# A softmax in layer 0: key tiles added in pairs by DMAs, half of the sums on TensorE, reciprocals with the queries on partitions

## The chip, the cores and the metric

The kernel runs on one core of a Trainium2 chip. The metric is the device time of one execution in microseconds (us). The kernel before was run three times: 3317.89, 3320.54 and 3327.8 us, median 3320.54. One further execution was profiled; its times are the ones told below.

A core has five engines that run their own streams of instructions in order and wait for each other through semaphores: TensorE (PE; its weight loads are listed as PEld), VectorE (DVE), ScalarE (ACT), GpSimd (POOL) and SyncE (SP), which here issues DMAs.

## The reference, cut to what matters

Two layers on 8 images of 256 channels and 32 x 32 pixels. Layer 0 is an attention over the 1024 pixels with a 3x3 depthwise convolution of the values beside it, and then a gated feed-forward part with another depthwise convolution and a filter in 8x8 Fourier blocks. Layer 1 is a causal attention and a mixture of 8 experts. The change lies in layer 0's attention:

```
def _attention(x, ...):
    B, Cc, H, W = x.shape
    N = H * W                                     # 1024 pixels
    qkv = _bn(_conv1x1(x, qkv_w), ...)
    qkv = qkv.reshape(B, NH, 2 * KD + HD, N)      # 4 heads, 32 + 32 + 64 channels
    q, k, v = (qkv[:, :, :KD], qkv[:, :, KD:2 * KD], qkv[:, :, 2 * KD:])
    attn = jnp.einsum('bhkn,bhkm->bhnm', q, k) * SCALE
    attn = jax.nn.softmax(attn, axis=-1)
    out = jnp.einsum('bhdm,bhnm->bhdn', v, attn).reshape(B, Cc, H, W)
    pe = _bn(_dwconv3(v_img, pe_w), ...)
    return _bn(_conv1x1(out + pe, proj_w), ...)
```

So each output is a sum over the keys of exponentials times values, divided by the sum of the same exponentials.

## The kernel before, in words

**Attention of one image** (`attend`, L724). The scores are computed transposed: keys on partitions, queries along the row. The 1024 queries go in 4 chunks of 256 (QC), the keys in 8 tiles of 128; a chunk and a tile make one step of the loop, 32 an image, 256 in all. A step does this:

- PE multiplies the keys with the queries of each head into PSUM tile `s`, 128 x 4 heads x 256 (L793). Queries and keys are split in a high and a low part, and four combinations are stacked along the partitions in `qst` and `kst`.
- ScalarE takes the exponential into `pT` (L795), without a shift by the maximum; a test at the end of the layer tells whether that was safe.
- For the tile before, `product` (L732) multiplies `pT` with the values, 8 matmuls of 32 columns each into `po`, and with a column block of ones, 4 matmuls of 32 columns into `sums`. Four column groups lie side by side in the array, so the sums of a head come out repeated on 32 partitions.

After the 8 tiles of a chunk `close` (L750) copies `po` to `pu` and `sums` to `ss` (ScalarE), and leaves a list of steps that are taken one by one in the following steps of the loop: `invert` takes the reciprocal of all 128 x 256 elements of `ss` on VectorE, `split` copies it into a high part on ScalarE and subtracts on GpSimd for the low part, and `spread` multiplies high and low part with a selection matrix on PE (4 matmuls), so that each channel has its head's reciprocal (`rb`), then multiplies `pu` by it and adds the result to `o` on VectorE. The steps of an image's last chunk are taken in `finish` (L808).

**The rest of layer 0** runs woven into this. `main_of(i)` (L1050) gives the stream of image i: the second norm of image i-1 and the Fourier part (`spectrum`) of image i-2, woven with the first steps of `attend(i)`; then `attend(i)` woven with the norm, queries and keys of image i+1 (`queries_keys`); then `stack(i+1)`, the values of i+1 (`values`) woven with `finish(i)` and the Gelus of i-1; then the projection (`project`). Beside it, `together` (L415) lays a side stream by a ratio of estimated microseconds: `hidden`, whose 3x3 convolution is done by `tap` (L561), one `scalar_tensor_tensor` on VectorE for each of 8 taps and each channel group, with PE's `ph` and ScalarE's copies into the padded tiles `hpad`. PE, ScalarE, VectorE and GpSimd are wrapped in `InOrder`, so that each one's instructions stand in the order in which the program makes them. The DMAs are SyncE's, and a scheduler places them.

**Buffers.** `pT` has 2 buffers, `s` 2 of two PSUM banks, `po` and `sums` one each. `hi` and `lo` of queries and keys have a buffer each; `stack` (L672) copies them within SBUF by 32 DMAs of 128 KB an image, 32 partitions each.

Of the kernel before, what the change touches and what calls it, by code (L numbers as in the profile page):

```python
# [9 lines left out]
F32 = mybir.dt.float32  # L10
# [45 lines left out]
NVEC = _n  # L56

# [17 lines left out]
def conv_attn_hybrid_kernel(  # L75
# [29 lines left out]

    vec = const.tile([P, NVEC], F32, name="vec")
    nc.sync.dma_start(vec, vecs)

    def col(name, i=0, n=1):
        o, w = _VOFF[name]  # L110
        assert i + n <= w
        return vec[:, o + i : o + i + n]
# [319 lines left out]
    with ExitStack() as l0:  # L432
# [78 lines left out]
        for k in range(KC):  # L511
# [8 lines left out]
        pick_r = wpool.tile([P, NH // 2, P], F32R, name="pick_r")  # L520
        pickr = one.tile([P, NH, HD], F32, tag="full", name="pickr", bufs=2)
        nc.gpsimd.memset(pickr, 0.0)
        nc.gpsimd.affine_select(
            out=pickr, in_=pickr, compare_op=ALU.not_equal, fill=1.0, base=0,
            pattern=[[-KD, NH], [0, HD]], channel_multiplier=1,
        )
# [3 lines left out]
        pick_n = wpool.tile([2 * nq, nq, P], F32R, name="pick_n")  # L530
        pickn = one.tile([2 * nq, nq, P], F32, tag="full", name="pickn", bufs=2)
        nc.gpsimd.memset(pickn, 0.0)
        for half in range(2):
            nc.gpsimd.affine_select(
                out=pickn, in_=pickn, compare_op=ALU.not_equal, fill=1.0, base=-nq * half,
                pattern=[[-1, nq], [0, P]], channel_multiplier=1,
            )
# [8 lines left out]
        def padded(name):  # L546
            p = one.tile([P, H + 2, W + 2], F32, tag=name, name=name)
            nc.gpsimd.memset(p, 0.0)
            return p

# [3 lines left out]
        def interior(p, h):  # L554
            r = H // 2
            return p[:, 1 + h * r : 1 + (h + 1) * r, 1 : 1 + W]
# [4 lines left out]
        def tap(dst, p, w, k):  # L561
            src = p[:, k // 3 : k // 3 + H, k % 3 : k % 3 + W]
            dve.scalar_tensor_tensor(rows(dst), src, w[:, k : k + 1], rows(dst), ALU.mult, ALU.add)
# [5 lines left out]
        def rms_norm(b, wname, xn):  # L569
# [38 lines left out]
            def apply(h):  # L608
                rT = rT_of.pop(h)
                rb = ps_m.tile([P, HALF], F32, tag="mm", name="rbn")  # L610
                for i in range(nq):
                    pe.matmul(rb[:, i * P : (i + 1) * P], pick_n[:, i, :], rT, start=True, stop=True)
                hs = slice(h * HALF, (h + 1) * HALF)
                for k in range(KC):
                    dve.scalar_tensor_tensor(xn[:, k, hs], t[b][:, k, hs], col(wname, k), rb, ALU.mult, ALU.mult)
# [36 lines left out]
        def queries_keys(b):  # L652
# [7 lines left out]
            for g in range(2):  # L660
                hi = one.tile([P, N], F32R, tag=f"hi{g}", name="hi")
                lo = one.tile([P, N], F32, tag=f"lo{g}", name="lo")
                bias = qkv_o[:, g : g + 1]

                def take(hs, pq):
                    act.activation(hi[:, hs], pq, AF.Identity, bias=bias)
                    dve.scalar_tensor_tensor(lo[:, hs], pq, bias, hi[:, hs].bitcast(F32), ALU.add, ALU.subtract)

                yield from qkv_group(b, g, take)
                att[b][g] = (hi, lo)  # L670

        def stack(b):  # L672
            for g in range(2):
# [3 lines left out]
                for r in range(4):  # L677
                    src = (hi, lo, hi, lo)[r] if g == 0 else (hi, hi, lo, lo)[r]
                    for hd in range(NH):
                        nc.sync.dma_start(  # L680
                            st[r * KD : (r + 1) * KD, hd, :].bitcast(F32), src[hd * KD : (hd + 1) * KD, :].bitcast(F32)
                        )
# [31 lines left out]
        def v_conv(b):  # L714
            o = att[b]["o"] = one.tile([P, KC, N], F32, tag="o", name="o")
            for g in range(KC):
                mid = vpad[g][:, 1 : 1 + H, 1 : 1 + W]
# [6 lines left out]
        def attend(b):  # L724
# [7 lines left out]
            def product(po, sm, j, pT):  # L732


                for pair in range(NH // 2):
                    for i in range(4):
# [7 lines left out]
                        )  # L744
                for hd in range(NH):
                    pe.matmul(
                        sm[hd * KD : (hd + 1) * KD, :], ones[:, :KD], pT[:, hd, :], start=(j == 0), stop=(j == nj - 1)
                    )

            def close(c, po, sm):  # L750
                pu = two.tile([P, NH // 2, QC], F32, tag="pu", name="pu", bufs=1)
                act.copy(pu, po)
                ss = two.tile([P, QC], F32, tag="ss", name="ss", bufs=1)
                act.activation(ss, sm, AF.Copy, accum_out=accs[:, 0, b, c : c + 1])
                r = two.tile([P, QC], F32, tag="sr", name="sr", bufs=1)
                rh = two.tile([P, QC], F32R, tag="rh", name="rh", bufs=1)
                rl = two.tile([P, QC], F32R, tag="rl", name="rl", bufs=1)
                qs = slice(c * QC, (c + 1) * QC)

                def invert():  # L760
                    dve.reciprocal(r, ss)

                def split():
                    act.activation(rh, r, AF.Copy, accum_out=accs[:, 1, b, c : c + 1])
                    pool.tensor_sub(rl, r, rh.bitcast(F32))

                def spread():
                    rb = ps_m.tile([P, NH // 2, QC], F32, tag="mm", name="rb")
                    for pair in range(NH // 2):
                        pe.matmul(rb[:, pair, :], pick_r[:, pair, :], rh, start=True, stop=False)  # L770
                        pe.matmul(rb[:, pair, :], pick_r[:, pair, :], rl, start=False, stop=True)
                    o = att[b]["o"][:, :, qs]
                    dve.tensor_mul(pu, pu, rb)
                    dve.tensor_add(o, o, pu)

                return [None, invert, None, split, None, None, spread]
# [7 lines left out]
            late = None  # L784
            for c in range(N // QC):
                qs = slice(c * QC, (c + 1) * QC)
                po = ps_o.tile([P, NH // 2, QC], F32, tag="po", name="po")
                sm = ps_o.tile([P, QC], F32, tag="sm", name="sums")
                for j in range(nj):
                    ks = slice(j * P, (j + 1) * P)  # L790
                    s = ps_s.tile([P, NH, QC], F32, tag="s", name="s")
                    for hd in range(NH):
                        pe.matmul(s[:, hd, :], kst[:, hd, ks], qst[:, hd, qs], start=True, stop=True)  # L793
                    pT = two.tile([P, NH, QC], F32, tag="pT", name="pT")
                    act.activation(pT, s, AF.Exp)  # L795
                    if late:
                        product(*late[:4])
                        if late[2] == nj - 1:
                            todo = close(c - 1, *late[:2])
                    late = (po, sm, j, pT)  # L800
                    later()
                    yield 1.75
            product(*late)
            todo = close(c, po, sm)
            att[b]["rest"] = todo
            yield 1.3

        def finish(b):  # L808
            for step in att[b]["rest"]:
# [45 lines left out]
        def group_on_pe(b, n):  # L855
# [15 lines left out]
            for h in range(2):  # L871
                pc = ps_m.tile([P, HALF], F32, tag="mm", name="pc")
                for k in range(9):
                    r0 = h * r + k // 3
                    pe.matmul(
                        pc, diag[:, k, :], pad[:, r0 : r0 + r, k % 3 : k % 3 + W], start=(k == 0), stop=(k == 8)
                    )
# [260 lines left out]
    wm = ctx.enter_context(tc.tile_pool(name="wm", bufs=1))  # L1138
    wrs = wm.tile([P, KC, NE], F32, name="wrs")
# [650 lines left out]
```

## Time and profile before

| what | value |
|---|---|
| median of 3 runs | 3320.54 us |
| profiled execution, its own time | 3326.09 us |
| its span, first to last instruction | 3324.3 us |
| PE busy | 3108.8 us, 94% of the span |
| VectorE busy | 2395.9 us, 72% |
| ScalarE busy | 1417.6 us, 43% |
| GpSimd busy | 328.9 us, 10% |
| mean granted clock of TensorE | 0.969 |
| DMA, mean over the span | 34 GB/s |
| `sums` matmuls | 2048 records, 158.8 us busy |
| `po` matmuls of layer 0 | 4096 records, 276.5 us busy |
| `s` matmuls of layer 0 | 1024 records, 217.9 us busy |
| exponentials `pT<-s` | 256, 1.024 us each |
| reciprocals `sr<-ss` | 32, 1.749 us each |

How to read it: the profile's page gives the busy time of each engine, the span in 40 slices, and groups of instructions by operation and tiles, each with its count, busy time, mean length and the idle time of the engine just before it. The timeline lists instructions in order of time; in brackets stands how long the engine had been idle and what released it. Matmuls are pipelined and their ends are modelled, so two matmuls' lengths overlap: what a matmul costs is read from one start to the next. Of a matmul in full 32-bit precision the trace holds two records, of one in the rounded form (`s`, `rb`, `tr`) one. The granted clock is the share of TensorE's clock that the chip let through. Layer 0 ends at about 1480 us of the span, its last attention at 1283 us.

### The profile page before, as it was taken

The page shows a single profiled execution, that of the slowest core. Times are in us where ns is not written, and L with a number is a line of the kernel's source. Part 1 is how long each engine was busy: PE and PEld are TensorE (multiplying, and loading weights), DVE is VectorE, ACT ScalarE, POOL GpSimd, SP SyncE. Part 2 cuts the span into 40 slices and gives each one's busy share as a digit, 9 for nine tenths or more (in the row PEclk, how much of TensorE's full clock was granted, in tenths as well). Part 3 has the DMA queues.
Part 4 walks back from the last instruction along what each step waited for, and adds up shares of the span by engine and source line. Part 5 has one row for each costly group of instructions (what it writes and reads, how often), then busy time and mean ns, then how long its engine had stood idle before and what let it go on. Part 6 is the DMA issues. An engine that isn't in the chain of part 4 may idle for free.

```text
span 3324.3 us, 43278 instructions
## 1 busy us (share of the span) xinstructions
PE 3108.8 (94%) x17366; PEld 2108.0 (63%) x17366; DVE 2395.9 (72%) x3710; ACT 1417.6 (43%) x2185; POOL 328.9 (10%) x530
## 2 busy tenths in 40 slices
PE   6998999999999998769999998999999999999999
PEld 4554646464656555345556666687878777878787
DVE  2369788878787887744554444688888877888887
ACT  2545454555454544313333332344444444444443
POOL 1120101020202010001222222400000000000000
PEclk9989999999999999879999999899999999999999
DMA  4112020202020200030111101100000000000000
GB/s 121 29 24 51 26 52 26 51 27 51 27 51 26 52 14 7 16 134 13 51 47 43 39 26 45 45 25 21 20 20 20 24 18 26 23 20 26 13 7 13
DMA packets 42918, 113.85 MB, mean 34 GB/s; under 512 B 6406, under 2 KB 14550, under 8 KB 38870
## 3 DMA queue, kind: packets, MB, share of 16 engines
q1 hardware_dynamic: 42710, 111.01, 11.0%
q8 instruction: 139, 2.28, 0.3%
q14 instruction: 69, 0.57, 0.1%
HBM read 43.61 MB, written 33.82 MB: 23 GB/s over the span
## 4 chain that ended last, share of the span: by engine, by line
PE 50%; DVE 4%; ACT 1%; POOL 1%; issue 0%; DMA 0%; POOLq 0%; ACTq 0%; SPq 0%; DVEq 0%
PE pm L69 12%; PE pa L69 12%; PE q L69 11%; PE s L69 5%; PE po L69 3%; PE pv L69 2%; PE pk L69 2%; DVE zt L69 1%; DVE nm L69 1%; PE tpt L69 1%; DVE pr L69 1%; PE tp L69 1%; ACT pr L69 1%; PE tpz L69 1%; PE pw L69 1%
## 5 line engine op out<-in xcount | busy, mean ns | idle before, releaser
L69 ACT ACTIVATE h<-h,bn_o,bn_s 128x512 f32<-128x512 f32 x384 | 308.7, 813 | 632.5 <-DVE h L69 632.4
L69 DVE SCALAR_TENSOR_TENSOR conv<-hpad,vec,conv 128x1024 f32<-128x1024 f32 x256 | 331.4, 1300 | 14.7 <-ACT conv L69 8.9
L69 DVE SCALAR_TENSOR_TENSOR x<-hpad,vec,x 128x1024 f32<-128x1024 f32 x248 | 321.6, 1300 | 23.5 <-ACT x L69 17.4
L69 ACT ACTIVATE pT<-s 128x1024 f32<-128x1024 f32 x256 | 261.6, 1024 | 150.3 <-PE s L69 150.1
L69 PE MATMUL pm<-h,w 128*128 128x512 f32 (+1 forms) x768 | 318.1, 523 | 0.0
L69 PE MATMUL po<-pT,vT 128*32 128x256 f32 x4096 | 276.5, 388 | 6.5 <-ACT pT L69 4.8
L69 PE MATMUL ph<-xn,piw 128*128 128x512 f32 x512 | 246.1, 608 | 3.1 <-DVE gf L69 1.1
L69 PE MATMUL s<-kk,z 128*128 128x512 f32 x512 | 242.4, 601 | 0.6 <-DVE pr L69 0.6
L69 PE MATMUL s<-qst,kst 128*128 128x256 f32 x1024 | 217.9, 335 | 6.1 <-DMA kst<-lo 5.9
L69 PEld LDWEIGHTS s<-qst,kst 128*128 128x128 f32 x1024 | 147.8, 192 | 88.8 <-issue 72.2
L69 PEld LDWEIGHTS pm<-h,w 128*128 128x128 f32 x768 | 146.7, 191 | 75.6 <-issue 62.1
L69 DVE TENSOR_TENSOR h<-h,wb 128x1024 f32<-128x1024 f32 x128 | 156.8, 1225 | 43.2 <-ACT h L69 43.2
L69 DVE TENSOR_TENSOR h<-pa,first 128x512 f32<-128x512 f32 x128 | 88.3, 690 | 134.9 <-PE pa L69 131.4
L69 DVE SCALAR_TENSOR_TENSOR o<-vpad,pe_w,o 128x1024 f32<-128x1024 f32 x128 | 163.3, 1281 | 24.1 <-ACT o L69 21.2
L69 ACT ACTIVATE hpad<-ph,pi_o 128x512 f32<-128x512 f32 x126 | 87.0, 691 | 211.7 <-PE ph L69 207.2
L69 DVE TENSOR_TENSOR h<-h,first 128x256 f32<-128x256 f32 x384 | 164.3, 428 | 13.2
L69 PEld LDWEIGHTS po<-pT,vT 128*32 128x32 f32 x4096 | 107.7, 109 | 88.7 <-ACT pT L69 8.3
L69 PEld LDWEIGHTS ph<-xn,piw 128*128 128x128 f32 x512 | 90.8, 190 | 108.9 <-issue 92.1
L69 PE MATMUL sums<-pT,ones 128*32 128x256 f32 x2048 | 158.8, 382 | 0.0
L69 PE MATMUL pz<-pow__118,hid 128*128 128x256 f32 x512 | 129.8, 408 | 29.1 <-DVE hid L69 29.1
L69 PE MATMUL pa<-tz,ws 128*128 128x256 f32 x512 | 156.0, 387 | 0.0
L69 PE MATMUL pa<-ze,w 128*128 128x256 f32 x512 | 153.8, 383 | 0.0
(258 smaller groups left out, 5940.3 us busy)
## 6 DMA issues: line engine op xcount, KB each, us to landing
t<-in_x_dram SPq DMA_DIRECT2D x8, 1024.0 KB, 7.5
qst<-hi SPq DMA_DIRECT2D x64, 128.0 KB, 2.3
qst<-lo SPq DMA_DIRECT2D x64, 128.0 KB, 2.3
kst<-hi SPq DMA_DIRECT2D x64, 128.0 KB, 2.3
kst<-lo SPq DMA_DIRECT2D x64, 128.0 KB, 2.3
td<-t SPq DMA_DIRECT2D x8, 1024.0 KB, 3.8
t<-td SPq DMA_DIRECT2D x8, 1024.0 KB, 4.9
ze<-zd SPq DMA_DIRECT2D x16, 512.0 KB, 4.1
```

The costliest lines, as they stand in the source:

```text
L69: return self._tc.keep_in_program_order(method(*args, **kwargs))
```

## The change: what it does

In layer 0's attention the exponentials of two neighbouring key tiles (2k and 2k+1) are added by a DMA that accumulates: GpSimd issues it one step after the odd tile's exponential, destination the even tile, source the odd one. The values are multiplied with each tile as before, ahead of the add; the ones are multiplied with the added tile alone, two steps after the odd tile's step (`total`). So the sums take 4 matmuls every second step. `pT` gets five buffers for this.

The close of a chunk is new: PE transposes the sums in two blocks, so that the queries lie on the partitions, VectorE takes the reciprocal of 128 x 8 elements out of PSUM, ScalarE copies them in place and accumulates for the test, GpSimd splits them into high and low part; two steps on PE transposes the parts back into 8 rows; one step on two matmuls with an 8-row selection matrix spread them over the channels. For the last chunk of an image the last sums themselves are taken in `finish`.

To make room, `hi` and `lo` have one buffer for queries and keys; they are written to HBM (`part`) as soon as they are made, and `stack` reads them from there by 8 DMAs an image. The padded tiles lose a column, the vector of constants for the experts is loaded after layer 0, and the selection matrix of the norms is kept as one column and broadcast.

```
-            def product(po, sm, j, pT):
+            def product(po, j, pT):
...
+            def total(c, j, pT):
+                if j == 1:
+                    of[c] = {"sm": ps_o.tile([P, QC], F32, tag="sm", name="sums")}
+                sm = of[c]["sm"]
                 for hd in range(NH):
                     pe.matmul(
-                        sm[hd * KD : (hd + 1) * KD, :], ones[:, :KD], pT[:, hd, :], start=(j == 0), stop=(j == nj - 1)
+                        sm[hd * KD : (hd + 1) * KD, :], ones[:, :KD], pT[:, hd, :], start=(j == 1), stop=(j == nj - 1)
                     )
+                if j == nj - 1:
+                    ss = of[c]["ss"] = two.tile([P, QC], F32, tag="ss", name="ss", bufs=1)
+                    act.activation(ss, sm, AF.Copy, accum_out=accs[:, 0, b, c : c + 1])
+                    todo.extend(close(c, of.pop(c)))
...
-                def invert():
-                    dve.reciprocal(r, ss)
-
-                def split():
-                    act.activation(rh, r, AF.Copy, accum_out=accs[:, 1, b, c : c + 1])
-                    pool.tensor_sub(rl, r, rh.bitcast(F32))
+                def turn():
+                    tp = ps_m.tile([P, nt, P], F32, tag="mm", name="tps")
+                    for i in range(nt):
+                        pe.transpose(tp[:, i, :], of["ss"][:, i * P : (i + 1) * P], ident)
+                    r = small.tile([P, nt, NH], F32, tag="sr", name="sr", bufs=2)
+                    dve.reciprocal(r, tp[:, :, ::KD])
+                    flat = r.rearrange("p a b -> p (a b)")
+                    act.activation(flat, flat, AF.Copy, accum_out=accs[:, 1, b, c : c + 1])
+                    rs = of["rs"] = small.tile([P, nt, 2, NH], F32, tag="rsp", name="rs", bufs=2)
+                    pool.tensor_copy(rs[:, :, 0, :].bitcast(F32R), r)
+                    pool.tensor_sub(rs[:, :, 1, :].bitcast(F32R), r, rs[:, :, 0, :])
+
+                def back():
+                    tr = ps_m.tile([2 * NH, QC], F32, tag="mm", name="trs")
+                    for i in range(nt):
+                        pe.transpose(tr[:, i * P : (i + 1) * P], of["rs"][:, i].rearrange("p a b -> p (a b)"), ident)
+                    of["rT"] = small.tile([2 * NH, QC], F32R, tag="rsT", name="rsT", bufs=2)
+                    act.copy(of["rT"], tr)
 
                 def spread():
                     rb = ps_m.tile([P, NH // 2, QC], F32, tag="mm", name="rb")
                     for pair in range(NH // 2):
-                        pe.matmul(rb[:, pair, :], pick_r[:, pair, :], rh, start=True, stop=False)
-                        pe.matmul(rb[:, pair, :], pick_r[:, pair, :], rl, start=False, stop=True)
+                        pe.matmul(rb[:, pair, :], pick_r[:, pair, :], of["rT"], start=True, stop=True)
+                    dve.tensor_mul(pu, pu, rb)
                     o = att[b]["o"][:, :, qs]
-                    dve.tensor_mul(pu, pu, rb)
                     dve.tensor_add(o, o, pu)
 
-                return [None, invert, None, split, None, None, spread]
+                return [None, turn, None, back, spread]
...
+            def added(n):
+
+                if n >= 0 and n % 2:
+                    pool.dma_start(tiles[n - 1], tiles.pop(n), accum_op=ALU.add)
+
+            def behind(n):
+
+                if n >= 0:
+                    product(po_of[n // nj], n % nj, tiles[n])
+                    if n % nj == nj - 1:
+                        c = n // nj
+                        pu = pu_of[c] = two.tile([P, NH // 2, QC], F32, tag="pu", name="pu", bufs=1)
+                        act.copy(pu, po_of.pop(c))
+                if n >= 3 and n % 2:
+                    total((n - 3) // nj, (n - 2) % nj, tiles.pop(n - 3))
...
+            for n in range(last + 1):
+                c, j = divmod(n, nj)
...
+                pT = two.tile([P, NH, QC], F32, tag="pT", name="pT", bufs=5)
+                act.activation(pT, s, AF.Exp)
+                behind(n - 1)
+                added(n - 1)
+                tiles[n] = pT
+                later()
+                yield 1.75
+            behind(last)
+            added(last)
             att[b]["rest"] = todo
+            todo += [None, lambda: total(last // nj, nj - 1, tiles.pop(last - 1))]
...
-                att[b][g] = (hi, lo)
+                parts = att[b][g] = [dram.tile([P, N], F32, tag=f"part{g}{r}", name="part", bufs=2) for r in range(2)]
+                for part, src in zip(parts, (hi, lo)):
+                    nc.sync.dma_start(part, src.bitcast(F32))
...
-                    for hd in range(NH):
-                        nc.sync.dma_start(
-                            st[r * KD : (r + 1) * KD, hd, :].bitcast(F32), src[hd * KD : (hd + 1) * KD, :].bitcast(F32)
-                        )
+                    nc.sync.dma_start(
+                        st[r * KD : (r + 1) * KD].bitcast(F32), src.rearrange("(h k) n -> k h n", k=KD)
+                    )
```

## The prediction

> **What bounds the kernel now.** I read the page's 40 slices first, then the groups of instructions kept apart by shape, then the timeline of single stretches, and last the DMA issues. All times are of the profiled execution (3326.09 us, span 3324.3); it lies 5.55 us above the median of the runs shown, 3320.54.
>
> The slices: a digit is the busy tenth of 83 us.
> ```profile
> PE   6998999999999998769999998999999999999999
> DVE  2369788878787887744554444688888877888887
> PEclk9989999999999999879999999899999999999999
> ```
> Layer 0 is the first 16 slices (to about 1310 us). TensorE is full there, VectorE at seven to eight tenths. The timeline of PE inside image 3's attention (start, length, operation, count) shows how full:
> ```profile
> 549.21 0.74 PE L69 MATMUL s<-qst,kst 128*128 128x256 f32 x4
> 549.88 1.07 PE L69 MATMUL po<-pT,vT 128*32 128x256 f32 x16
> 550.77 0.61 PE L69 MATMUL sums<-pT,ones 128*32 128x256 f32 x8
> 551.31 0.74 PE L69 MATMUL s<-qst,kst 128*128 128x256 f32 x4
> ```
> Each start follows the one before with no idle mark: a key tile costs 0.67 (s) + 0.89 (po) + 0.54 (sums) = 2.10 us, read from start to start, since the lengths overlap. So in the loop the end is set by PE's stream, and VectorE waits for it (in image 3 for 5.5 us at `pu`, 3.3 us at `lo`). At the end of an image it is the other way round. PE there, then VectorE:
> ```profile
> 650.16 0.66 PE L69 MATMUL tpv<-ident,vfull 128*128 128x128 f32 x4 [1.93 <-ACT vfull L69]
> 652.57 0.58 PE L69 MATMUL rb<-rh,pick_r 128*128 128x256 f32 x1 [1.75 <-ACT rh L69]
> ...
> 654.29 9.39 PE L69 MATMUL pp<-o,projw 128*128 128x512 f32 x16
> ```
> ```profile
> 647.60 1.75 DVE L69 RECIPROCAL sr<-ss 128x256 f32<-128x256 f32 x1
> 649.26 2.38 DVE L69 SCALAR_TENSOR_TENSOR conv<-hpad,vec,conv 128x1024 f32<-128x1024 f32 x2
> ...
> 658.40 0.68 DVE L69 TENSOR_TENSOR pu<-pu,rb 128x512 f32<-128x512 f32 x1
> ```
> The sums were ready at 636.3, VectorE came to the reciprocal 11.3 us later, and PE waits behind it. The stretches by window (PE, PEld, DVE, ACT, POOL busy, granted clock, DMA) show what follows:
> ```profile
> 645.00:650.00 5.00, 2.83 (x13) 1.35 (x11) 3.85 (x5) 5.00 (x9) 0.00 (x0) 1.00 0.91 206
> 650.00:655.00 5.00, 2.75 (x9) 1.84 (x10) 4.96 (x6) 2.99 (x7) 0.84 (x1) 0.72 0.91 207
> 655.00:660.00 5.00, 5.00 (x8) 1.96 (x7) 4.89 (x6) 0.00 (x0) 0.00 (x0) 0.60 0.07 15
> ```
> After PE's idle time the granted clock falls, and the first `pp` records start 0.85 us apart instead of 0.43.
>
> **The change, part by part.**
>
> *Sums.* 128 of 256 groups go. A group is 0.545 us to the next start, of which 8 x 0.055 = 0.44 are its records; the other 0.1 us is the switch to full-width matmuls, which then follows `po`. So 128 x 0.44 = -56 us (-70 if the switch went too). All of it is in the PE-bound loop.
>
> *Closing a chunk.* PE today: four `rb`, 0.57 us from first start to the next group. After: two transposes of `ss` (four `tpv` take 0.44, so 0.22), two of eight rows (`tr`: 0.03 to 0.11 each), two `rb` (0.24), up to three switches of 0.1: 0.5 to 1.0, taken as 0.75. 32 x 0.18 = +6 us (-2 to +13). VectorE loses 32 reciprocals of 1.75 us and gets 32 of some 0.2 (the 128x1 form takes 0.16). In the loop VectorE waits for PE, so this is worth nothing there, but it keeps VectorE ahead of a faster PE: it had 3.3 us of idle time at `lo`, loses 6.5 us to PE's gain and regains 5.
>
> *ScalarE's new wait.* The step `turn` puts on ScalarE a copy that waits for PE's transposes and then for VectorE's reciprocal; behind it stands the next `exp`, for which PE's `po` waits. Today two key tiles lie between reciprocal and copy. From the starts above the next `exp` has some 0.7 us to spare. In 14 of 32 closes VectorE was already waiting for `ss` (idle at `sr`), else it was late by one tap (1.3 us) or more: +5 us (0 to 16).
>
> *End of an image.* In the order of the changed program the last sums come after the first value transposes and the last reciprocal stands four taps later in VectorE's queue, with two taps (2.6 us) before `pu`, where today two `hid` products and six taps follow it. Between reciprocal and `pu` now lie a ScalarE copy (0.4), two GpSimd steps (0.2 to 1 each), transposes, a copy (0.26), `rb` (0.34) and five hand-overs of some 0.1: about 3.0 us. That is 0.4 us more than its cover; and PE, which today starts `pp` 4.1 us ahead of `pu`, starts it beside `pu`. Image 3, with PE 6.5 us early (16 x 0.44 less three closes) and one reciprocal gone from VectorE's full stretch: `pu` at 658.4 - 6.5 - 1.55 + 0.4 = 650.8, `pp` from 650.7 (today 654.29), 9.2 us long if the clock falls as today, so to 659.9 (today 663.5); a 0.6 us wait of `pz` goes. The image gains 4.2 to 4.5 of 6.5: 8 x 2 = +16 us (0 to 30).
>
> *The adding DMAs.* 128 of 512 KB, GpSimd's queue. No accumulating DMA and no DMA from GpSimd is in the trace. PE waits for the landing before each remaining sums group; behind it stands everything on PE. The time allowed, by the timeline: from the end of the odd tile's `exp` to the start of the sums two tiles on, less the two groups that go (0.88). Tile 7 of image 3: `exp` ends at 551.07, tile 9's sums start at 557.05, so 5.1 us. Over the 15 pairs of each image that have this in the loop: least 4.4, median 8.7; 14 of 120 under 5.5, 37 under 7, 70 under 9. With a stall widening the next window, a landing of 5 / 5.5 / 6 / 7 / 8 / 9 / 10 us costs 1 / 6 / 13 / 34 / 59 / 89 / 133 us in all. The nearest rows for the landing:
> ```profile
> qst<-hi SPq DMA_DIRECT2D x64, 128.0 KB, 2.3
> ze<-zd SPq DMA_DIRECT2D x16, 512.0 KB, 4.1
> zd<-z SPq DMA_DIRECT2D x2, 512.0 KB, 3.1
> ```
> A plain 512 KB takes 3.1 to 4.1. Adding reads a second operand: eight 4 KB rows a DMA engine at 0.16 to 0.30 us a packet (loads of `x`; copies into `qst`) = 1.3 to 2.4. GpSimd's issue lies between SyncE's 0.4 and the 2.08 us of GpSimd's slowest small operation beside taps; its pow takes 1.0 alone. Ends: 4.8 and 8.6. I take 3.1 + 1.3 + 1.0 = 5.4, hence +6 us, by the row of the same size out of SBUF. GpSimd's queue: its chain for a norm (seven operations, up to 7 us beside taps) and the two split steps of a close stand ahead of an issue; the pairs there have 8.8 us or more. Behind an issue stand those chains; their readers come two steps later.
>
> *What else uses the DMA engines.* `td<-t` and the next `x` keep them 0.6 busy from 546 to 554, on the very pairs with 6.8 and 5.1 us: +1 us an image, +6. The stack's copies begin as the last pair is added; that pair has some 9 us.
>
> The Trainium skill bears on the landing. DMA: Bandwidth & Descriptors, "Anatomy of one DMA", fits 2.0 us + bytes / 436e3 for GpSimd's DMAs, and Collectives: The Full Stack explains that an add costs a second read, not ALU time: 4.4 us, by which the stalls would be about 0. Against the change speaks SBUF — State Buffer, "Who interferes with whom": a VectorE instruction with two SBUF inputs shuts out GpSimd instructions that read SBUF, and descriptors are written by GpSimd. Here a GpSimd TENSOR_SCALAR of four columns takes 0.19 us free of taps and 1.23 beside them. The page spares GpSimd work that only writes; if issuing were held up by a tap all the same, 1.3 us more give 6.7 us and +27.
>
> *The rest, at nothing.* Queries and keys reach the stack through HBM, in 12 DMAs an image instead of 32. From image 1 on the copies have from 633 to the first `s` at 669.6 for 20 us of transfers. In image 0 they are on the path: PE waits 5.9 us for `kst<-lo` today, behind 32 issues of 0.6 us; fewer issues and one more hop, -5 to +5. The second vector load and the expert folds move to the start of layer 1, where ScalarE waits 20.7 us for a load. Narrower padding changes no element count.
>
> Sum: -56 + 6 + 5 + 16 + 6 + 6 = -17 us, 3309 on the profiled execution's scale, **3303** on the median's.
>
> **Rivals.** *The whole gain*: landing under 5 us, the end of the image hidden: -56 + 6 = -50, 3270 on the median's scale. For it: the plain rows; against it: PE's start of `pp`. *Eaten up*: the end of each image gives back all (30), ScalarE's wait 16: within 10 us of no change, 3320. For it: the 11.3 us by which VectorE is late there; against: it also loses a reciprocal. *Slower*: the landing. PE waits in the dense pairs of each image. Before stalls the sum is -23 with the collisions; a landing over 6.5 us undoes it (interpolated in the tally above), at 9 us the time is 3320.5 - 23 + 89 = 3387, at 8 us 3357. For it: no row shows an add, GpSimd is slowed by taps, 64 MB more go through engines that other copies use. Against: half the windows are over 8.7.
>
> **How the numbers follow.** Forecast 0.40, whole gain 0.12, eaten up 0.15, slower 0.33. A measurement tells 0.3% (10 us) from no change. Faster: 0.12 and nine tenths of the forecast, 0.48; within: 0.04 and most of the eaten-up case, 0.16; slower 0.36. The range 3275 to 3372 leaves out about 0.05 below and 0.15 above (landings over some 8.5 us). The forecast's own range is 3285 to 3315.
>
> **What would show it.** The `sums` group halves and starts follow at 0.67 + 0.89 + 0.1; idle marks on `sums` name the adding DMA only in the dense pairs and total some 12 us; `rb` at the end of an image is followed by `pp` at the time of `pu`; `exp` waits for `sr` in few closes. A landing over 6.5 us, or idle time before every sums group, makes the forecast wrong.

## The result, and the profile after

The changed kernel takes 3428.68 us (median of 4 runs, 3422.41 to 3439.2) against 3320.28 us for the kernel before on the same chip: a ratio of 1.0326, 95% interval 1.0294 to 1.0357. It is 108 us slower; the forecast was 3303, the range ended at 3372. The profiled execution took 3439.2 us, its span is 3437.5 us. It is the slowest of the four, so differences read from the profiles can be some 10 us larger than those of the medians.

The slices of the page (PE, VectorE, granted clock, DMA share; a slice is now 86 us):
```profile
PE   5988888988888889877999999899999999999999
DVE  1348867676767678673545444478888877888887
PEclk9989999989898999988999999899999999999999
DMA  4635243334434344103000010100000000000000
```
Layer 0 shows it at once: PE, full before, is at eight tenths, VectorE fell as well, and the clock dips within the stretch. Neither engine is the bound any more; something else lets both wait. The window from the first `s` of image 0 to the last `pp` of image 7 puts numbers on it (stretch, PE, PEld, VectorE, ScalarE, GpSimd busy, granted clock, DMA share, GB/s), before and then after:
```profile
71.10:1305.40 1234.30, 1158.71 (x9421) 676.05 (x9422) 978.22 (x918) 635.29 (x949) 149.68 (x228) 0.96 0.14 35
```
```profile
79.50:1419.20 1339.70, 1164.47 (x8461) 658.82 (x8462) 921.67 (x917) 643.36 (x981) 289.15 (x388) 0.91 0.42 93
```
PE has 960 records fewer and is busy 6 us longer, because the mean clock fell from 0.96 to 0.91; the trace's clock records give 100 us at half clock in this stretch before and 236 us after. The rest is idle time of PE, 76 us before (1234.30 less 1158.71) and 175 after. The waits of PE after, over layer 0 (waiter, releaser, sum, times, longest):
```profile
PE sums L70 <- DMA pT<-pT: 87.5, 26, 8.0
PE trs L70 <- POOL rs L70: 25.6, 8, 7.4
PE s L70 <- DMA kst<-part: 13.8, 1, 13.8
PE tpv L70 <- ACT vT L70: 12.9, 6, 2.2
```
So PE waits for 26 adding DMAs, 87.5 us: 50.3 in the loops over the key tiles, 36.6 at the ends of the images, 0.6 behind the last. That is not because every add is slow. The page's DMA issues (size, median time to landing):
```profile
pT<-pT POOLq DMA_DIRECT2D x128, 512.0 KB, 4.7
qst<-part SPq DMA_DIRECT2D x32, 512.0 KB, 10.6
kst<-part SPq DMA_DIRECT2D x32, 512.0 KB, 18.4
```
The median landing, 4.7 us, is even below the 5.4 that was taken. The waits sit in a few places, the same in each image.

**In the loop.** Image 2: ScalarE, GpSimd, PE, from the timeline of each.
```profile
438.75 1.02 ACT L70 ACTIVATE pT<-s 128x1024 f32<-128x1024 f32 x1
440.85 0.26 ACT L70 ACTIVATE y<-ms,eps_rms 128x4 f32<-128x4 f32 x1 [1.08 <-PE ms L70]
```
```profile
441.20 1.86 POOL L70 TENSOR_TENSOR a<-y,mhalf 128x4 f32<-128x4 f32 x1 [5.35 <-ACT y L70]
443.14 1.72 POOL L70 TENSOR_TENSOR y<-y,a 128x4 f32<-128x4 f32 x2
...
447.44 1.25 POOL L70 CAST r<-a 128x4 fp32r<-128x4 f32 x1
448.76 0.20 POOL L70 TENSOR_TENSOR r<-a,r 128x4 fp32r<-128x4 f32 x1
449.25 1.84 POOL L70 DMA_DIRECT2D pT<-pT  x2 [0.28 <-issue]
```
```profile
447.15 1.07 PE L70 MATMUL po<-pT,vT 128*32 128x256 f32 x16
453.97 1.08 PE L70 MATMUL sums<-pT,ones 128*32 128x256 f32 x8 [5.75 <-DMA pT<-pT]
454.98 1.22 PE L70 MATMUL s<-qst,kst 128*128 128x256 f32 x4
456.13 1.94 PE L70 MATMUL po<-pT,vT 128*32 128x256 f32 x16
```
The odd tile's exponential ended at 439.8, so its add could have been issued then. In GpSimd's order the norm's chain stands ahead of it; the chain begins when ScalarE's `y` is there and takes 7.8 us beside the taps. Two adds are then issued back to back at 449.25, 9.5 us late. The first lands 4.7 us on, PE has waited 5.75 us, and the matmuls behind the wait (`po` 1.94 long instead of 1.07) run at half clock.

**At the end of an image.** PE in image 3, and what the DMA queues do there (DMA issues of the window 686 to 716):
```profile
694.44 0.60 PE L70 MATMUL tpv<-ident,vfull 128*128 128x128 f32 x4
698.79 1.08 PE L70 MATMUL sums<-pT,ones 128*32 128x256 f32 x8 [3.75 <-DMA pT<-pT]
...
714.69 0.59 PE L70 MATMUL trs<-ident,rs 128*8 128x128 f32 x2 [2.38 <-POOL rs L70]
715.73 0.79 PE L70 MATMUL rb<-rsT,pick_r 8*128 8x256 f32 x2 [0.45 <-ACT rsT L70]
```
```profile
kst<-part SPq DMA_DIRECT2D x4, 512.0 KB, 18.3
qst<-part SPq DMA_DIRECT2D x3, 512.0 KB, 11.2
pT<-pT POOLq DMA_DIRECT2D x1, 512.0 KB, 12.3
```
The last pair's add shares the DMA engines with the next image's stack and takes 12.3 us. By the records of the single DMAs it takes 12.3 to 14.3 in images 0 to 6, and 5.4 in image 7, which no stack follows.

Where the time of the profiled executions stands, stage by stage, as differences to the kernel before in us (all eight images; "loop" from the first `s` to the last `po`, "end" from there to the first `pp`, "rest" `pp` and the way to the next `s`), with the runs of the next section:

| kernel | first `s` | loops | ends | rest | PE waits on `sums` | at half clock |
|---|---|---|---|---|---|---|
| before | | | | | 0 | 100 |
| after | +8.4 | +42.9 | +77.5 | -15.1 | 87.5 | 236 |
| e1 no adds | +8.0 | -28.3 | +24.9 | -14.3 | 0 | 147 |
| e4 last pair on PE | +7.7 | +23.4 | +27.3 | -18.0 | 51.4 | 147 |
| e9 earlier issue | +9.0 | -10.4 | +78.0 | -13.1 | 49.5 | 196 |
| e10 both, split on VectorE | +8.6 | -9.9 | +14.7 | -14.2 | 14.8 | 132 |
| e11 no adds, split on VectorE | +7.0 | -36.4 | +10.6 | -14.5 | 0 | 103 |
| e12 as e10, one pair more on PE | +8.9 | -25.2 | +14.2 | -15.7 | 3.7 | 114 |

### The profile page after: what moved, and what is told of

It reads as the page before. It is cut to its first block, busy times and chain, and to the rows that moved or that the text cites. A ratio compares the mean times of both kernels' runs of the same rounds, so it can differ in the third digit from the quotient of the medians.

```text
span 3437.5 us, 41399 instructions
## 1 busy us (share of the span) xinstructions
PE 3113.6 (91%) x16406; PEld 2091.3 (61%) x16406; DVE 2339.7 (68%) x3710; ACT 1426.3 (41%) x2218; POOL 467.5 (14%) x691
## 4 chain that ended last, share of the span: by engine, by line
PE 47%; DVE 4%; ACT 1%; POOL 1%; issue 1%; SPq 0%; DMA 0%; ACTq 0%; POOLq 0%; DVEq 0%
PE pm L70 12%; PE pa L70 11%; PE q L70 11%; PE s L70 4%; PE po L70 3%; PE pk L70 2%; PE pv L70 2%; DVE nm L70 1%; DVE zt L70 1%; DVE pr L70 1%; DVE st L70 1%; ACT pr L70 1%; PE tpt L70 1%; PE tp L70 1%; PE tpz L70 1%
## 5 line engine op out<-in xcount | busy, mean ns | idle before, releaser
L70 PE MATMUL po<-pT,vT 128*32 128x256 f32 x4096 | 290.1, 403 | 9.1 <-ACT pT L70 7.1
L70 PE MATMUL s<-qst,kst 128*128 128x256 f32 x1024 | 227.4, 347 | 13.8 <-DMA kst<-part 13.8
L70 PEld LDWEIGHTS s<-qst,kst 128*128 128x128 f32 x1024 | 154.7, 202 | 99.7 <-issue 88.6
L70 POOL DMA_DIRECT2D pT<-pT x128 | 112.1, 889 | 535.6 <-ACT pT L70 372.1
L70 PE MATMUL sums<-pT,ones 128*32 128x256 f32 x1024 | 86.9, 414 | 87.7 <-DMA pT<-pT 87.5
L70 PE MATMUL q<-t,ws 128*128 128x256 f32 x512 | 152.5, 380 | 0.8 <-DVE t L70 0.8
## 6 DMA issues: line engine op xcount, KB each, us to landing
qst<-part SPq DMA_DIRECT2D x32, 512.0 KB, 10.6
```

Of the source, the lines that this page charges most:

```text
L70: return self._tc.keep_in_program_order(method(*args, **kwargs))
```

## The experiments

### Which part costs it: e1 to e4

**e1** leaves the adding DMAs out.
```
-                    pool.dma_start(tiles[n - 1], tiles.pop(n), accum_op=ALU.add)
+                    tiles.pop(n)
```


> The changed kernel with the 128 adding DMAs left out and nothing put in their place: the sums then hold every second key tile alone, so the output is not the reference's. PE's work is that of the changed kernel. Theory (the adds cost it: PE waits 87 us at `sums` for them in layer 0, and the granted clock is halved for 255 us there instead of 153): with no add the idle marks on `sums` go, the half-clock time comes back to about 160 us, and the time is about 3300 (3290 to 3320). Rival A (the stack's way through HBM is the cost): 3390 to 3420, as the first `s` of each image stays late. Rival B (the new way from the sums to the reciprocals is the cost): 3370 to 3410, the 10 us longer stretch from the last `po` to the first `pp` of images 0 to 6 stays.

Measured: 3316.77 us, ratio 0.9985 (0.9975 to 0.9994). The adds cost 112 us; both rivals are out. The two profiles show what they are: from the first `s` to the last `pp` the changed kernel takes 123 us more than e1, of which 85 are idle time of PE and 38 are more busy time for the same 8461 records (1164.47 us against 1126.82), and 89 us more of it are at half clock. (The expectation counted half clock up to 1500 us of the span, which takes in a part of layer 1; the table ends at the last `pp`.) But the time lies at the upper end of what was expected: without the adds the change gains 5 us (by the ratio), not the 29 that the prediction's other terms come to. What ate those 24 is asked in e2 and e11.

**e2** keeps all sums on PE and has no adds.
```
+                for i, pT in enumerate(pTs):
+                    for hd in range(NH):
...
-                if n >= 0 and n % 2:
-                    pool.dma_start(tiles[n - 1], tiles.pop(n), accum_op=ALU.add)
+                return
...
-                    total((n - 3) // nj, (n - 2) % nj, tiles.pop(n - 3))
+                    total((n - 3) // nj, (n - 2) % nj, (tiles.pop(n - 3), tiles.pop(n - 2)))
```


> The changed kernel with the adding DMAs left out and the sums taken over both tiles of each pair on PE (two groups of 4 matmuls every second step): it keeps five buffers, the stack through HBM and the new close. Theory (the adds): the 56 us of PE come back on top of the run without adds, so 3345 to 3370, about 70 below the changed kernel. Rival A (HBM stack) and rival B (the close): 3430 to 3480, the loss stays and the PE work is added.

Measured: 3350.14, ratio 1.009 (1.0073 to 1.0108). As the theory said. Two things follow. Halving the sums is worth 33 us (3350.14 - 3316.77), not 56: with them gone the trace has 35 us more at half clock and 9 us more idle time. And against e3, which has the detour through HBM, the rest of the change, the new close above all, costs 21 us.

**e3** is the kernel before with the stack through HBM, by 8 DMAs an image and with one buffer each for `hi` and `lo`.
```
+                parts = att[b][g] = [dram.tile([P, N], F32, tag=f"part{g}{r}", name="part", bufs=2) for r in range(2)]
+                for part, src in zip(parts, (hi, lo)):
+                    nc.sync.dma_start(part, src.bitcast(F32))
...
+                    nc.sync.dma_start(
+                        st[r * KD : (r + 1) * KD].bitcast(F32), src.rearrange("(h k) n -> k h n", k=KD)
+                    )
```


> The kernel before with one part of the change alone: one buffer each for `hi` and `lo`, their way through HBM and the stack in 8 DMAs an image. Theory (the adds): 3322 to 3335, of it some 8 us before the first `s`, nothing from image 1 on. Rival A (the stack's way is the cost): 3380 to 3430, with the first `s` of each image 5 to 10 us later. Rival B (the close): 3320 to 3325.

Measured: 3329.19, ratio 1.0015 (1.0004 to 1.0026). The first `s` is 7.5 us later, the first `s` of image 1 only 1.4; the detour is no cause.

**e4** sums the last pair of each image on PE; `total` takes a list of tiles for it.
```
+                for i, pT in enumerate(pTs):
+                    for hd in range(NH):
...
-                if n >= 0 and n % 2:
+                if n >= 0 and n % 2 and n < last:
...
-            todo += [None, lambda: total(last // nj, nj - 1, tiles.pop(last - 1))]
+            todo += [None, lambda: total(last // nj, nj - 1, (tiles.pop(last - 1), tiles.pop(last)))]
```


> The changed kernel, but the last pair of each image (8 of 128) is not added by DMA; PE sums both of its tiles (4 matmuls more an image, 3.5 us in all). Theory (at the end of an image the last add shares the DMA engines with the stack's copies, lands after 12 to 14 us, and PE waits): the wait on `sums` at the end of images 0 to 6 goes, 4 to 8 us each, and with it a part of the half-clock time after it: 3375 to 3400. Rival A (HBM stack) and rival B (the close): the wait moves to `kst` or to `trs`, 3420 to 3430.

Measured: 3365.64, ratio 1.0139 (1.0117 to 1.0162): 63 us for 8 of 128 adds, more than the theory gave. PE at the end of image 3:
```profile
660.78 0.60 PE L70 MATMUL tpv<-ident,vfull 128*128 128x128 f32 x4
661.31 1.07 PE L70 MATMUL sums<-pT,ones 128*32 128x256 f32 x16
662.32 3.70 PE L70 MATMUL pq<-xn,qkvw 128*128 128x512 f32 x8
...
674.92 0.59 PE L70 MATMUL trs<-ident,rs 128*8 128x128 f32 x2 [2.37 <-POOL rs L70]
```
The sums follow at once, and `pq` runs at full clock (3.70 for eight, 5.97 after); the wait does not move elsewhere. The ends fall from +77.5 to +27.3. The loops fall by 20 too, although PE waits as long on `sums` there (51.4 us, 50.3 in the changed kernel): that part goes with the clock, at half for 147 us instead of 236. The 2.4 us for `rs` stay.

### What holds the adds in the loop: e5 to e9

**e5** takes the sums one step later.
```
-                if n >= 3 and n % 2:
-                    total((n - 3) // nj, (n - 2) % nj, tiles.pop(n - 3))
+                if n >= 4 and n % 2 == 0:
+                    total((n - 4) // nj, (n - 3) % nj, tiles.pop(n - 4))
...
+            todo.append(lambda: total(last // nj, nj - 3, tiles.pop(last - 3)))
```


> The changed kernel with the ones multiplied with an added pair one step later (three steps after the odd tile's instead of two); no buffer more, no other work. Theory (in the loop the landing is late against its window): 2.1 us more for each landing. The waits on `sums` in the loop (3 to 6 us in one or two places of each image, some 50 us with the clock after them) go; the wait at the end of an image for the last pair stays: 3375 to 3395. Rival (the adds cost because their 64 MB of traffic slow the other transfers or the engines' operands, not because PE waits for the landing): 3415 to 3430.

Measured: 3381.99, ratio 1.0192 (1.0175 to 1.0209). The time falls into the theory's range, but not for its reason: PE's waits on `sums` fall to 11.2 us, at the ends of the images too, where the theory had them stay, and waits on `po` come up instead, 33.8 us (9.0 in the changed kernel). e7 shows why.

**e6** splits the reciprocal on VectorE.
```
-                    act.activation(flat, flat, AF.Copy, accum_out=accs[:, 1, b, c : c + 1])
+                    seen = small.tile([P, nt * NH], F32, tag="seen", name="seen", bufs=2)
+                    act.activation(seen, flat, AF.Copy, accum_out=accs[:, 1, b, c : c + 1])
...
-                    pool.tensor_copy(rs[:, :, 0, :].bitcast(F32R), r)
-                    pool.tensor_sub(rs[:, :, 1, :].bitcast(F32R), r, rs[:, :, 0, :])
+                    dve.tensor_copy(rs[:, :, 0, :].bitcast(F32R), r)
+                    dve.tensor_sub(rs[:, :, 1, :].bitcast(F32R), r, rs[:, :, 0, :])
```


> The changed kernel with the reciprocal's split in a high and a low part on VectorE straight behind the reciprocal (two more instructions of 8 columns there), so that GpSimd has no step of a close ahead of an adding DMA, and ScalarE's copy for the test goes to a tile of its own. Theory (GpSimd's queue holds a DMA's issue behind the close's two steps, which wait for ScalarE and VectorE): the waits of 5.7 us in the loop, one or two an image, go, and the 2.4 us for `rs` ahead of `trs` at the end of an image shrink to under 1: 3385 to 3405. Rival (the landing itself is late, whatever the queue): the loop's waits stay, only the end gains 8 x 2: 3410 to 3420.

Measured: 3399.33, ratio 1.024 (1.0223 to 1.0257). Again the number fits and the reason does not: of the five waits in the loops of images 2 to 6 four are still there, 5.7 us each, and PE waits 80.6 us on `sums`. The gain is at the ends (+77.5 to +60.6; `trs` waits 0.3 us in images 2 to 6, where it waited 2.4) and 18 us in the loops, where the waits on `sums` fall by 4 us only (50.3 to 46.4). So it is not the close that holds the issue; what stands in GpSimd's stream at these places is the norm's chain (the timeline above).

**e7** takes both edits, later sums and the last pair on PE.

> The changed kernel with both edits: sums one step later, and the last pair of each image summed on PE without an add. Theory: nothing waits for a landing any more, so the time is that of the run without adds (3317) and 3.5 us for PE's sums: 3315 to 3330. Rival (traffic): still 20 us or more above that, 3340 to 3365, with no idle marks on `sums`.

Measured: 3376.91, ratio 1.0173 (1.0156 to 1.019): both wrong, and 11 us worse than e4 alone. PE waits 3.0 us on `sums` and 40.1 on `po` (9.0 after). ScalarE shows why:
```profile
601.01 0.26 ACT L70 CAST rT<-tr 8x128 fp32r<-8x128 f32 x1 [0.73 <-PE tr L70]
606.45 1.94 ACT L70 ACTIVATE pT<-s 128x1024 f32<-128x1024 f32 x2 [5.18 <-DMA pT<-pT]
```
With five buffers, an added pair that is held a step longer leaves the next exponential no buffer but that of a source tile whose add has not landed. The wait moves from `sums` to the exponential and so to `po`. No run gave `pT` a sixth buffer, so later sums with buffers enough stay untried.

**e8** adds to e7 the split on VectorE and takes the last sums at the end of the loop.
```
-            todo.append(lambda: total(last // nj, nj - 3, (tiles.pop(last - 3),)))
-            todo += [None, lambda: total(last // nj, nj - 1, (tiles.pop(last - 1), tiles.pop(last)))]
+            total(last // nj, nj - 3, (tiles.pop(last - 3),))
+            total(last // nj, nj - 1, (tiles.pop(last - 1), tiles.pop(last)))
```


> As the run before it (sums one step later, last pair on PE), but the last pair is summed at the end of the loop and not two steps into the end of the image, and the split is on VectorE straight behind the reciprocal. Theory (of the 4 us that the end of an image is longer even without adds, some 2.4 are GpSimd's two steps and the rest the later sums): 3290 to 3310, faster than both kernels. Rival (the end is set by ScalarE's and VectorE's other work there): 3315 to 3330, as the run before it.

Measured: 3343.39, ratio 1.0082 (1.0066 to 1.0099). That is above both ranges. The ends come to +12.5, against +27.8 in e7, so moving the close's steps does shorten them; but the loops keep the exponentials' waits for a buffer (30.1 us on `po`).

**e9** puts the issue one step earlier into GpSimd's stream; beside that only the place changes where the program's list drops the odd tile.
```
-                    pool.dma_start(tiles[n - 1], tiles.pop(n), accum_op=ALU.add)
+                    pool.dma_start(tiles[n - 1], tiles[n], accum_op=ALU.add)
...
-                    product(po_of[n // nj], n % nj, tiles[n])
+                    product(po_of[n // nj], n % nj, tiles.pop(n) if n % 2 else tiles[n])
...
+                tiles[n] = pT
                 behind(n - 1)
-                added(n - 1)
-                tiles[n] = pT
+                added(n)
...
-            added(last)
```


> The changed kernel with each adding DMA put into GpSimd's stream one step earlier, at the end of the odd tile's own step and not of the next one; what the DMA itself waits for (the odd tile's exponential, the even tile's product) is the same. Theory, mended after the last runs (an issue stands in GpSimd's order behind the seven steps of a norm, which start when ScalarE has `y` and take 8 us beside taps; two pairs are then issued back to back up to 10 us late): the waits of 5.7 us in the loop go, the loops of images 2 to 6 come back to 125 to 131 us, and the last pair of an image is issued about 2 us earlier: 3365 to 3395. Rival (the landing is late against a window of two steps, whoever issues it): the loop's waits stay, 3415 to 3430.

Measured: 3383.91, ratio 1.0188 (1.0162 to 1.0213). 45 us less, all of it in the loops (+42.9 to -10.4 in the profiles); the ends stay (+78.0). GpSimd at the same place of image 2:
```profile
431.30 0.94 POOL L70 DMA_DIRECT2D pT<-pT  x1 [7.75 <-ACT pT L70]
432.90 1.04 POOL L70 TENSOR_TENSOR a<-y,mhalf 128x4 f32<-128x4 f32 x1 [0.66 <-ACT y L70]
...
435.46 0.20 POOL L70 TENSOR_TENSOR r<-a,r 128x4 fp32r<-128x4 f32 x1
438.82 0.94 POOL L70 DMA_DIRECT2D pT<-pT  x1 [3.16 <-ACT rT L70]
```
The add now stands ahead of the chain and leaves as its exponential ends; the waits of 5.7 us are gone from every image, and of the 50.3 us on `sums` in the loops 15.2 are left. For the long waits the place in the stream was the cause, not the landing and not the window: this is the one edit that moves no work and no wait.

### What is left: e10 to e12

**e10** has the earlier issue, the last pair on PE at the end of the loop, and the split on VectorE. **e11** is the changed kernel without adds, with the split on VectorE and the last sums at the end of the loop.

> The issue one step earlier, the last pair of each image summed on PE at the end of the loop, and the reciprocal's split on VectorE. Theory (waits for landings are all that the adds cost): the time of the next run, which has no adds, and 3.5 us for PE's sums, 3295 to 3315, faster than both kernels by 0.2 to 0.8%. Rival (64 MB of traffic cost engines or other transfers time even where nothing waits for a landing): 10 us or more above the next run and those 3.5 us.

> The changed kernel with the adding DMAs left out (the sums hold every second key tile alone, so the output is not the reference's), the split on VectorE and the last sums at the end of the loop: what the change could give at most with its new close. Theory (without adds the end of images 0 to 6 is 4 us longer than before, 2.4 of it GpSimd's two steps and some of it the later last sums): 3317 less 7 x 3, about 3290 to 3305. Rival (the end is set by ScalarE there, which the last transposes wait for): 3310 to 3320.

Measured: e10 3315.58, ratio 0.9977 (0.9961 to 0.9994); e11 3293.93, ratio 0.9926 (0.9908 to 0.9944). e11 is in the theory's range: the close's two GpSimd steps and the later last sums were worth 23 us against e1. e10 is 22 us above e11 where 3.5 were expected, so waits for landings were not all gone: PE still waits 14.8 us on `sums`, half of it, 2.2 to 2.6 us each, at one pair of images 2 to 4, whose add meets the copies of `t` and `x` (landing 6.2 to 8.4 us in images 2 to 5). And 29 us more are at half clock, 17 of them behind a stretch that waits for no add (last section). By its number e10 fits the rival, traffic; e12 bears on that.

**e12** has e10's edits and sums that pair on PE too, in images 2 to 7.
```
+            on_pe = (7, N // QC * nj - 1) if b >= 2 else (N // QC * nj - 1,)
...
-                if n >= 0 and n % 2:
-                    pool.dma_start(tiles[n - 1], tiles.pop(n), accum_op=ALU.add)
+                if n >= 0 and n % 2 and n not in on_pe:
+                    pool.dma_start(tiles[n - 1], tiles[n], accum_op=ALU.add)
...
-                    total((n - 3) // nj, (n - 2) % nj, tiles.pop(n - 3))
+                    total((n - 3) // nj, (n - 2) % nj, (tiles.pop(n - 3),) + ((odd[n - 2],) if n - 2 in on_pe else ()))
```


> As the run with the early issue, the last pair on PE and the split on VectorE, and in images 2 to 7 the pair of key tiles 6 and 7 of the first chunk is summed on PE as well: its add meets the copies of `t` to HBM and of the next `x`, lands after 6 to 8.4 us and lets PE wait 1.1 to 2.6 us in images 2 to 6. Theory: those 9.8 us of waits go and the half clock behind them, less 6 x 0.44 for PE's sums: 3295 to 3310, faster than the kernel before. Rival (traffic costs where nothing waits too, so the loss shows elsewhere): 3312 to 3320.

Measured: 3302.82, ratio 0.9948 (0.9934 to 0.9961): faster than the kernel before. It is 9 us above e11, about what PE's sums that e11 does not do (8 and 6 groups of 0.44, 6.2 us) and the waits left (3.7) come to. So for 114 adds, 57 MB, nothing is left that traffic would have to explain; the runs spread over 13.6 us (e12) and 9.2 us (e11), so a few microseconds of it are not ruled out. VectorE's taps of 128 x 1024 elements in layer 0 last 1.28 us in e12 and 1.30 before, so they are not slowed. The loop of image 3, before and in e12 (the window view, columns as above):
```profile
505.90:635.00 129.10, 125.28 (x1130) 74.95 (x1133) 103.62 (x97) 64.94 (x97) 20.08 (x31) 1.00 0.05 19
```
```profile
501.00:626.40 125.40, 121.05 (x1007) 72.08 (x1011) 97.71 (x102) 65.61 (x100) 32.27 (x42) 0.99 0.39 91
```
DMA share 0.39 instead of 0.05, clock 0.99 instead of 1.00, PE 4.2 us less busy, VectorE 5.9 (shorter reciprocals and one tap less in the window), and the loop 3.7 us shorter.

## Why the prediction was wrong, step by step

**The landing** was taken as 5.4 us from the plain 512 KB copies. Right in the median (4.7, least 4.5; the 4.4 that the prediction gives beside it lies just below the least). GpSimd's issue took 0.85 to 0.94 us in 121 of 128 and 1.20 at most, so taps did not hold it up by the 1.3 us that the prediction weighed. The rival "slower through landing" had the right sign, but with a break-even at a landing of 6.5 us for every pair; what happened is a landing of 4.7 that starts late, or one of 12 to 14 in one place. Neither of the two signs that the prediction named for a wrong forecast appeared as such: the median landing stayed under 6.5 us, and only 26 of 128 sums groups waited.

**GpSimd's queue** is the step that failed first: "its chain for a norm (seven operations, up to 7 us beside taps) ... stand ahead of an issue; the pairs there have 8.8 us or more". Chain and window were about right (7.8 us; PE would have come to these sums 8.4 us after the exponential). But the chain was held against the window alone, and the landing, which follows it, left out: 7 + 5.4 is more than 8.8 by the prediction's own numbers. The chain also starts only when `y` is there, 1.4 us after the add was ready. Cost by e9: 45 us.

**"The stack's copies begin as the last pair is added; that pair has some 9 us"** failed too. The window was 9.1 us in images 2 to 6 (8.6 from the issue), as said, but the landing there is not the median: with 4 MB ahead and beside it, it is 12.3 to 14.3. The prediction had the 20 us of transfers and the share of busy DMA engines in hand and counted a collision only for `td` and `x`. Cost by e4: 63 us, net of the 3.5 us of sums that e4 adds. (45 and 63 were each taken out alone, and part of each is the clock; they need not add up.)

**The price of a wait.** The tally counted a stall as its length. e1 shows 112 us for 87.5 us of waits; in the profiles 38 us are PE's longer busy time, with more half clock behind the waits. The prediction had seen this at the end of an image and not carried it into the loop.

**`td` and `x`, +6**: right place, too small. The waits on `sums` that e12 takes away against e10 are 11.1 us, and the medians differ by 12.8 with 2.6 us of PE's sums put back. That would be some 15, an estimate, as e10's ten runs spread over 23 us.

**Sums, -56**: the arithmetic (0.44 a group) holds, the yield does not: 33 us by e2 and e1. The step taken for granted was that a stream with less work stays dense.

**Closing a chunk, +6 (-2 to +13)**: in the range, towards its upper end. At full clock `tps` takes 0.26 us to the next start in the mean, `trs` 0.23 (0.14 to 0.31, by what follows), `rb` 0.43, against 0.58 before: 0.34 each, 11 us.

**End of an image, +16**: mechanism right, size low. For image 3 the steps put the first `pp` 2.9 us later after the last `po` than before (3.6 us earlier against 6.5); without adds it is 4.0. GpSimd's two steps took 0.85 and 1.25 us beside taps, where 0.2 to 1 each was taken. With them on VectorE and the sums earlier (e11) it is 1.5.

**ScalarE's new wait, +5**: PE's waits at `po` rise from 6.4 us to 7.3 in e1 and 9.0 in the changed kernel, so little of it shows as idle time; no run tells it apart. **The rest, at nothing**: the detour through HBM held within 5 us (e3), with the first `s` 7.5 us later where -5 to +5 was given; the padding and the moved loads were not run alone.

The sum of what the forecast left out at the adds is 112 us; the other terms together were some 24 us too good, of which e11 gives 23 back by moving two small steps and the last sums; the time at half clock falls from 147 us in e1 to 103 with it, as before the change.

## What to carry to other kernels

When work moves to a DMA that an engine must issue, list what stands ahead of the issue in that engine's stream and add it to the landing before comparing with the window; the cheapest cure is often to move the issue, not the reader. Take the landing at each place from what else the DMA engines carry just then, not from the median, and leave the one or two pairs that collide on the engine they came from. Price a wait of TensorE with the half clock behind it, and look for the buffer that a longer lifetime takes away before giving a DMA more time.

## What the runs showed that was not expected

**The clock falls without a long gap, and by where the gap lies in time.** In e1 (no adds) around 390 us PE idles only 0.83 us ahead of a `po`, and then runs matmuls of one column, 16 records:
```profile
386.87 1.07 PE L70 MATMUL po<-pT,vT 128*32 128x256 f32 x16 [0.83 <-ACT pT L70]
387.87 0.38 PE L70 MATMUL trs<-ident,rs 128*8 128x128 f32 x2
388.09 2.11 PE L70 MATMUL ms<-mean,sq 128*128 128x1 f32 x16
```
```profile
385.00:390.00 5.00, 4.17 (x46) 3.06 (x39) 3.34 (x3) 3.09 (x5) 0.00 (x0) 0.95 0.00 0
390.00:395.00 5.00, 5.00 (x32) 2.82 (x33) 0.26 (x1) 2.21 (x4) 2.18 (x7) 0.50 0.00 0
395.00:400.00 5.00, 5.00 (x20) 2.38 (x23) 4.88 (x5) 1.55 (x3) 0.00 (x0) 0.52 0.00 0
```
PE counts as busy behind the gap and yet runs ten microseconds at half clock. The Trainium skill, TensorE: Matmul & The Clock Gate, section "Why this matters for your kernels", asks for no idle gap over about 3 us. Here a gap of 0.83 and two microseconds of one-column matmuls were followed by the same fall. But in images 3 and 5 of e1 the same instructions follow a gap of the same length, and the clock stays (image 3):
```profile
554.62 1.07 PE L70 MATMUL po<-pT,vT 128*32 128x256 f32 x16 [0.82 <-ACT pT L70]
555.62 0.38 PE L70 MATMUL trs<-ident,rs 128*8 128x128 f32 x2
555.84 1.84 PE L70 MATMUL ms<-mean,sq 128*128 128x1 f32 x16
```
```profile
555.00:560.00 5.00, 5.00 (x64) 3.52 (x52) 1.12 (x1) 3.05 (x6) 1.61 (x5) 1.00 0.01 3
```
What differs is the moment. In each of the 14 traces the granted clock changes only at points of a grid of 3.41 us, to within 0.1 us, so half clock lasts 3.4, 6.8, 10.2 or 13.7 us, seldom longer. The stretch above (a wait of 0.82 to 0.83 us, `po`, two transposes, the one-column matmuls) stands 40 times in eight of the traces, in images 2 to 6. Where the next point of the grid came 2.3 to 2.7 us after the start of `po`, 10.2 us of half clock followed, 10 times of 10; at 2.8 to 3.2 us, 3.4 us of it, 9 of 9; at 0 to 2.2 us, none, 21 of 21. So the same short wait costs nothing or ten microseconds at half clock by where it falls on the grid, and an edit that only shifts the stretch moves the time with it: e10 has 20.5 us of half clock behind these five stretches, e11 3.4, e12 23.9. Whether the gap alone would do, or the transposes and the one-column matmuls must follow it, stays open; no run took them away.

**The clock differs from run to run.** Ten runs of e10 lie between 3302.71 and 3326.01 us, and their mean clock goes with it: 0.970 for the two fastest, 0.964 and 0.965 for the three slowest.

**An accumulating DMA of 512 KB within SBUF**, issued by GpSimd, took 0.85 to 0.94 us to issue in most cases, 1.20 at most, and landed in 4.5 us with the engines free, 6.5 to 6.8 as the second of two issued back to back, 5.8 to 8.8 beside the copies of `t` and `x`, and 12.3 to 14.3 beside the stack's copies.
